# Zeroing the stacks of queries and keys on ScalarE instead of GpSimd in a two-layer attention kernel

## The chip, the cores and the metric

The kernel runs on one core of one Trainium2 chip, in one launch. The metric is device time in microseconds (us). The kernel before has a median of 918.5 us over 3 runs (918.21 to 922.14). The core's engines are named as in the profile: PE is TensorE's matmuls, PEld its weight loads, DVE is VectorE, ACT is ScalarE, POOL is GpSimd, SP is SyncE, whose queue issues the DMAs. Each engine works off its own instructions in the order in which they were written, and waits where an operand isn't there yet.

## The reference

Input `x` is 32 sequences of 256 tokens of 256 features, in float32. Two layers follow each other; each normalizes its input, attends, and modulates the outcome with a condition vector (512 features per sequence).

```python
# layer 0: linear attention, 8 heads of 32
xn = _ln(x, ln_w, ln_b)
q = softmax((xn @ Wq + bq).reshape(b, t, 8, 32), axis=-1)
k = softmax((xn @ Wk + bk + (1 - mask) * -1e6).reshape(b, t, 8, 32), axis=1)
v = ((xn @ Wv + bv) * mask).reshape(b, t, 8, 32)
att = einsum('bnhd,bnhl->bhdl', k, v)
y = einsum('bnhd,bhdl->bnhl', q, att)
# layer 1: softmax attention, 16 heads of 16
att = softmax(einsum('bnhl,bmhl->bnmh', q, k) + (1 - mask) * -1e6, axis=2)
y = einsum('bnmh,bmhl->bnhl', att, v)
# both, with their own weights
scale, shift = split(silu(emb) @ W_emb + b_emb)
x = x + silu(_ln(y, ln2_w, ln2_b) * (1 + scale) + shift) @ W_out + b_out
```

## The kernel before, in words

One function, `tile_two_layers`, first collects operations and then writes them out. `prepared()` lists the set-up: loading weights, folding the first normalization's weights into the projections, splitting float32 weights into a high and a low part (`w_high` on ACT, L305; `w_low` on DVE, L308), the modulation vectors, constants, and buffers that are filled once. `sequence(b)` lists the work of one of the 32 sequences (called batches here), in parts a (layer 0's attention), b (layer 0's output), c (layer 1's attention) and d (layer 1's output).

The order is written out by hand as numbers: `SET_UP` gives each set-up operation a place, `STARTS` each operation of a batch, to which `PERIOD` (26.2851) times the batch's number is added. `in_order` sorts all operations by place and runs them one after the other; an operation whose inputs or buffers aren't there yet is put off until they are. The places set the order of the instructions on every engine's queue. They are not clock times of a run.

Operations that stand near the change:

- `identity` (L264, POOL, place -708.56) makes the identity matrix `ident` and two small constants; `warmed` runs 16 transposes on PE with it; `identity_r` (L270 to L272, DVE) casts `ident` to `ident_r`, reduces it to `fold` and spreads that to `fold4`.
- `qk_zeros` (L507) fills one pair of stacks, `qs` and `ks`, with zeros; each is 128 partitions x 2048 float32 values. There are three pairs (`ROOM["qk"]`). The list in `SET_UP` goes by the order in which the operations are listed, but each `qk_zeros` takes the next pair when it runs, so the pair with the earliest place is the first to be used.
- `qk_made` (L512, places -52.44, 60.07, 77.11) then issues two DMAs from SP that write the constant rows into the pair's stacks (L515), and sets the pair free for use. In part c, the heads' queries and keys are copied by DMA into the other rows of a free pair (L991); rows that are not written stay zero, and the score matmuls (L1033, L1100) run over all of them.
- ACT's queue in the set-up: `w_high` of layer 0's output weights (`wout_hi`, place -439.51), `cond_tanh` (L425, place -332.9), `w_high` of layer 1's output weights (-231.47), and then the other `w_high` among the work of the first batches. DVE's queue there: `identity_r`, `token_terms` (L435, L436), one `w_rep` (L322, L323), `w_low` of layer 0's output weights (`wout_lo`, L308, reads `wout_hi`), the other `w_rep`, `bias_scaled` (L332). PE's `w_sums` (L345, L349) read the scaled bias and the spread rows of `w_rep`.
- The place 5.55 in ACT's queue lies between `split_high` of batch 0 (L752, place 4.18) and `k_kept` of batch 1 (L818, place 6.37). `k_kept` copies the turned keys of layer 0 into `kk`, which `attention` (L888, PE) reads; `k_sums` (L896) and `blocks` (L901) on DVE read its result, and `y_product` (L916, PE) reads theirs. After `k_kept` ACT has `high` and `whole` (L699, L703) of batch 3, and two `w_high`.

Of the kernel before, what the change touches and what calls it, by code (L numbers as in the profile page):

```python
# [10 lines left out]
F32 = mybir.dt.float32  # L11
# [5 lines left out]
P = 128  # L17
# [50 lines left out]
    identity_r=(-702.04,), load_bias=(-276.37,), load_bout=(-13.79, 53.66), load_cols=(-670.58,),  # L68
    load_cond=(-544.29,), load_emb=(-258.80, -217.52, -180.67, -207.44, -42.77, -14.95, -48.76, -2.89),
    load_masks=(-359.47,), load_w=(-291.77, -528.39, -390.22, -548.16, -39.72, -33.64, -88.51, -232.84),  # L70
    mask_terms=(-103.15,), p_made=(91.90, 5.63), qk_made=(-52.44, 60.07, 77.11), qk_zeros=(-61.21, -379.66,
    -674.55), qkp_made=(30.64,), terms0_store=(-141.84,), terms_rows=(-172.06,), terms_store=(-42.73,),
    terms_turn=(-333.70,), token_terms=(-574.41,), v0_made=(-369.51, -279.71), va_made=(-36.90, 52.97),
    w_high=(-50.10, -64.76, -198.98, -439.51, 25.73, 18.32, 14.13, -231.47), w_low=(-39.74, -58.97, -95.39,
    -307.80, 29.41, 24.14, 30.22, 4.56), w_rep=(-292.96, -366.10), w_scaled=(-76.66, -94.61, -210.46, 20.45,
# [89 lines left out]
def tile_two_layers(ctx: ExitStack, tc: tile.TileContext, a: dict, out: bass.AP):  # L165
# [11 lines left out]
    nc = tc.nc  # L177
    x = a["x"]
    B, S, D = x.shape
# [7 lines left out]
    NSLOT = NU * NC  # L187
# [4 lines left out]
    const = ctx.enter_context(tc.tile_pool(name="const", bufs=1))  # L192
# [8 lines left out]
    def f(ap):  # L201
        return ap.bitcast(F32)
# [6 lines left out]
    ident_r = const.tile([P, P], F32R, name="ident_r")  # L209
    fold = const.tile([P, B], F32, name="fold")  # L210
    one = const.tile([P, 1], F32, name="one")
    minus_half = const.tile([P, NBLOCK], F32, name="minus_half")
    fold4 = const.tile([P, P], F32, name="fold4")
    cols = const.tile([P, NCOL + 2 * NTOK], F32, name="cols")
# [26 lines left out]
    done = {}  # L241
# [11 lines left out]
    def prepared():  # L253
# [3 lines left out]
        def op(engine, time, run, *after, take=(), give=(), **more):  # L257
            ops.append(Op(engine, time, run, after, take, give, **(LATE.get(engine, {}) | more)))
            return ops[-1]
# [4 lines left out]
        def identity():  # L264
            make_identity(nc, ident)
            nc.gpsimd.memset(one, 1.0)
            nc.gpsimd.memset(minus_half, -0.5)

        def identity_r():
# [11 lines left out]

        o_cols = op("D", 0.3, load_cols)
        o = op("G", 0.9, identity)
        op("P", 0.11 * NWARM, warmed, o, take=("bank",), give=("bank",))
        done["ident"] = op("V", 0.13, identity_r, o)

# [153 lines left out]
        o = op("D", 0.3, load_bias)  # L440
# [17 lines left out]
        o = op("V", 0.2, token_terms, o_cols)  # L458
        o = op("P", 0.5, terms_turn, o, done["ident"], take=("bank",))
        o = op("V", 0.35, terms_rows, o, give=("bank",))  # L460
# [15 lines left out]
        o = op("D", 0.3, load_cond)  # L476
        o = op("A", 0.2, cond_tanh, o)
# [20 lines left out]
        o = op("D", 0.3, load_masks)  # L498
        o = op("V", 0.6, mask_terms, o)
# [7 lines left out]
        def qk_zeros():  # L507
            s.qk.append(qk_all.pop(0))
            for buf in s.qk[-1]:
                nc.gpsimd.memset(f(buf), 0.0)  # L510

        def qk_made():  # L512
            qk_bufs.append(s.qk.pop(0))
# [14 lines left out]
        o = op("G", 0.6, zero_one)  # L528
        o_stored = op("D", 0.3, zero_one_store, o)
        o_z = o_stored  # L530
        for n in range(ROOM["qk"]):
            o = op("G", 4.0, qk_zeros)
            o_z = op("D", 0.8, qk_made, o, o_z, give=("qk",))

        o_rep = norm_rows(1, o_cols)
# [630 lines left out]

    ctx.enter_context(tc.manual_schedule(engines=None))
    return in_order(prepared, [lambda b=b: sequence(b) for b in range(B)], ROOM)


# [67 lines left out]
```

## Time and profile before

| | |
|---|---|
| median of 3 runs | 918.5 us (918.21 to 922.14) |
| the profiled execution | 914.85 us, span 912.7 us |
| mean granted TensorE clock | 0.97 |
| PE busy | 864.9 us (95% of the span) |
| DVE busy | 813.5 us (89%) |
| ACT busy | 700.2 us (77%) |
| POOL busy | 692.4 us (76%) |
| the six zeroings on POOL, L510 | 1.80 to 1.82 us each; four from 1.80 to 8.84 us, two from 18.53 to 22.07 us |

The profile is that of one execution. The span is the time from its first to its last recorded instruction; the execution's own time is a little longer. A line of a timeline gives start and length in us, engine, source line, operation, the tile written and those read, the shape (partitions x elements) and how many were merged (x4); in brackets stands how long the engine was idle before and what ended it. The chain of waits is the work that ended last, followed backwards from the last instruction, at each step to what released it or to the instruction before it on its engine. In a table of stretches, each row gives the stretch, its length, the busy time of PE, PEld, DVE, ACT and POOL with their instructions, the granted TensorE clock (1.00 is full speed), the DMA engines' busy share and GB/s.

The page's slices (40 equal parts of the span, busy tenths) show where the time is filled and where it isn't:

```profile
PE   6878899999999999999999999999999999999973
DVE  6797989999999999999999999999999999999843
ACT  1365588788888898888888888888888888877762
POOL 5254567888888888988888888988888877775441
PEclk6799999999999999999999999999999999999985
```

The first four slices (about 91 us) and the last two are the start-up and the end; in between PE is busy nearly all the time.

### The profile page before, as it was taken

Reading aid. Unit: us, or ns where it says so; the run is one execution under the profiler, and the core shown is the slowest. Engines: PE = TensorE matmul, PEld = TensorE weight load, DVE = VectorE, ACT = ScalarE, POOL = GpSimd, SP = SyncE. Lnnn points to the kernel's source line nnn. Section 1 sums busy time; section 2 is a strip of 40 time slices with the busy share of each in tenths; the row PEclk is TensorE's granted clock in tenths of the full one; section 3 lists DMA queues with packets and bytes.
Section 4 is the critical chain, followed back from the end, with each engine's and each line's share of the span. In section 5 each row is a group of like instructions: output and inputs, shape, how many; then the busy total and the mean of one; then the engine's idle time right before and its main releaser. Section 6 shows DMA issues by size and latency. Waiting matters only on the chain.

```text
span 912.7 us, 25210 instructions
## 1 busy us (share of the span) xinstructions
PE 864.9 (95%) x9494; PEld 705.0 (77%) x9494; DVE 813.5 (89%) x2235; ACT 700.2 (77%) x1420; POOL 692.4 (76%) x893
## 2 busy tenths in 40 slices
PE   6878899999999999999999999999999999999973
PEld 3667787888888888888888888888888888877642
DVE  6797989999999999999999999999999999999843
ACT  1365588788888898888888888888888888877762
POOL 5254567888888888988888888988888877775441
PEclk6799999999999999999999999999999999999985
DMA  6302222322232222223222212332233221222200
GB/s 215 108 16 88 84 81 81 102 104 97 103 103 74 89 71 90 102 104 103 96 104 86 86 60 92 104 102 104 96 104 103 71 82 57 87 86 86 95 14 24
DMA packets 56767, 81.09 MB, mean 89 GB/s; under 512 B 5407, under 2 KB 30021, under 8 KB 56646
## 3 DMA queue, kind: packets, MB, share of 16 engines
q1 hardware_dynamic: 56646, 79.47, 25.4%
q8 instruction: 76, 1.25, 0.6%
q14 instruction: 45, 0.37, 0.1%
HBM read 19.52 MB, written 8.55 MB: 31 GB/s over the span
## 4 chain that ended last, share of the span: by engine, by line
PE 79%; DVE 15%; POOL 2%; issue 1%; ACT 1%; DMA 0%; POOLq 0%; DVEq 0%; ACTq 0%
PE bank L558 37%; PE bank L1122 12%; PE bank L1100 9%; PE bank L1033 8%; PE bank L565 5%; DVE mx L1044 5%; PE bank L916 3%; PE bank L814 1%; PE bank L888 1%; DVE st L591 1%; PE bank L650 1%; PE bank L349 1%; DVE th L746 1%; DVE ident_r L270 1%; DVE yb L1138 1%
## 5 line engine op out<-in xcount | busy, mean ns | idle before, releaser
L1044 DVE TENSOR_REDUCE mx<-bank 128x2 f32<-128x512 f32 x512 | 324.9, 673 | 15.0 <-PE bank L1033 14.7
L1113 ACT ACTIVATE p<-bank 128x512 f32<-128x512 f32 x512 | 270.2, 600 | 84.1 <-PE bank L1100 78.5
L558 PE MATMUL bank<-xh,w_hi 128*128 128x256 f32 x512 | 153.1, 299 | 0.1
L558 PE MATMUL bank<-xl,w_hi 128*128 128x256 f32 x512 | 144.3, 282 | 1.2 <-DVE xl L707 1.2
L558 PE MATMUL bank<-xh,w_lo 128*128 128x256 f32 x512 | 143.9, 281 | 0.0
L1122 PE MATMUL bank<-p,va 128*32 128x256 f32 x2048 | 140.0, 386 | 0.1
L558 PE MATMUL bank<-wout_hi,hp 128*128 128x256 f32 x512 | 112.9, 302 | 10.0 <-ACT hp L752 9.5
L982 POOL TENSOR_TENSOR qk_lo<-nrm,qk_hi 128x512 fp32r<-128x512 f32 x58 | 74.7, 1287 | 56.5 <-ACT nrm L978 56.5
L1100 PE MATMUL bank<-qs,ks 64*128 64x256 f32 x1024 | 109.0, 311 | 4.3 <-DMA qs<-m_row 3.1
L1033 PE MATMUL bank<-ks,qs 64*128 64x256 f32 x1024 | 105.4, 307 | 1.0 <-DVE mx L1044 0.3
L1100 PEld LDWEIGHTS bank<-qs,ks 64*128 64x128 f32 x1024 | 73.8, 187 | 37.0 <-ACT p L1113 22.6
L558 PEld LDWEIGHTS bank<-xh,w_hi 128*128 128x128 f32 x512 | 97.1, 190 | 5.1 <-DVE mx L1044 0.4
L558 PEld LDWEIGHTS bank<-xl,w_hi 128*128 128x128 f32 x512 | 97.3, 190 | 1.6 <-DVE xl L707 1.6
L558 PEld LDWEIGHTS bank<-wout_hi,hp 128*128 128x128 f32 x512 | 86.3, 196 | 15.6 <-ACT hp L752 10.1
L1033 PEld LDWEIGHTS bank<-ks,qs 64*128 64x128 f32 x1024 | 73.6, 185 | 31.3 <-issue 13.4
L558 PEld LDWEIGHTS bank<-xh,w_lo 128*128 128x128 f32 x512 | 96.9, 189 | 0.0
L613 POOL TENSOR_SCALAR nrm<-xt,mv,off 128x256 f32<-128x256 f32 x116 | 65.0, 571 | 29.0 <-DVE off L608 26.1
L1122 PEld LDWEIGHTS bank<-p,va 128*32 128x32 f32 x2048 | 55.0, 109 | 41.1 <-ACT p L1113 1.8
L728 POOL TENSOR_TENSOR xt<-xt,bout 128x512 f32<-128x512 f32 x64 | 82.5, 1288 | 3.1 <-DMA bout<-in_bout_dram 3.1
L756 POOL TENSOR_TENSOR hp<-th,hp 128x512 fp32r<-128x512 f32 x58 | 74.9, 1292 | 9.1 <-ACT hp L752 9.1
L558 PE MATMUL bank<-w_hi,xh 128*128 128x256 f32 x256 | 78.2, 305 | 0.0
L707 POOL TENSOR_TENSOR xl<-nrm,xh 128x512 fp32r<-128x512 f32 x58 | 73.6, 1288 | 4.3 <-ACT nrm L703 4.3
(138 smaller groups left out, 2153.9 us busy)
## 6 DMA issues: line engine op xcount, KB each, us to landing
ks<-qk_hi SPq DMA_DIRECT2D x64, 256.0 KB
qs<-qk_hi SPq DMA_DIRECT2D x64, 256.0 KB
xt<-in_x_dram SPq DMA_DIRECT2D x32, 256.0 KB
ks<-qk_lo SPq DMA_DIRECT2D x32, 256.0 KB
qs<-qk_lo SPq DMA_DIRECT2D x32, 256.0 KB
out_dram<-xt SPq DMA_DIRECT2D x32, 256.0 KB
mk<-t_dram SPq DMA_DIRECT2D x32, 128.0 KB
raw<-in_w_dram SPq DMA_DIRECT2D x8, 256.0 KB
```

The costliest lines, as they stand in the source:

```text
L558: nc.tensor.matmul(o, left, right, start=(n == 0), stop=(n == len(pairs) - 1))
L565: nc.tensor.transpose(ps[:, ds(c * S + t * P, P)], src[:, t, ts(c, P)], ident)
L613: (nc.vector if s.quick else nc.gpsimd).tensor_scalar(s.nrm[:, t, :], get()[:, t, :], s.mv[:, t, 1:2], s.off[:, t : t + 1], ALU.mult, ALU.add)
L707: engine.tensor_tensor(s.xp[1], s.whole, f(s.xp[0]), ALU.subtract)
L728: nc.gpsimd.tensor_tensor(s.x, s.x, bout[:, i : i + 1, :].to_broadcast([P, NT, D]), ALU.add)
L756: engine.tensor_tensor(s.hp[1], s.th, f(s.hp[0]), ALU.subtract)
L982: engine.tensor_tensor(s.qkp[1][:, :, c], s.qk_ps[c], f(s.qkp[0][:, :, c]), ALU.subtract)
L1033: nc.tensor.matmul(ps[w][:, ts(m, S)], s.qs[half(w), u, c, ts(m, P)], s.ks[half(w), u, c, :], start=True, stop=True,)
L1044: nc.vector.tensor_reduce(s.mx[:, :, w, u, c], halves(s.s_ps[0, c, u][w]), AX.X, ALU.max, negate=True)
L1100: nc.tensor.matmul(ps[w][:, ts(m, S)], s.ks[half(w), u, c, ts(m, P)], s.qs[half(w), u, c, :], start=True, stop=True,)
L1113: nc.scalar.activation(s.pt[c, u][:, w], s.s_ps[1, c, u][w], AF.Exp)
L1122: nc.tensor.matmul(s.yT_ps[c][32 * j : 32 * j + 32, ts(v, S)], s.va[:, m, 8 * c + 4 * v + j, :], s.pt[c, 2 * v + j // 2][:, j % 2, ts(m, S ...
```

## The change

The stacks are zeroed by ACT: `nc.scalar.copy` writes all 2048 columns of a stack from a new constant tile of one column, `nothing`, which POOL fills with zeros inside `identity`. `qk_zeros` becomes an operation of ACT's queue that needs `identity`; it has three new places in `SET_UP`, two of them near the set-up's start and one at 5.55. The operations around it, their places and the DMAs of `qk_made` stay.

```diff
@@ SET_UP
-    qk_zeros=(-61.21, -379.66, -674.55),
+    qk_zeros=(-650.21, -640.66, 5.55),
@@ tile_two_layers
     one = const.tile([P, 1], F32, name="one")
+    nothing = const.tile([P, 1], F32, name="nothing")
@@ identity
             nc.gpsimd.memset(one, 1.0)
+            nc.gpsimd.memset(nothing, 0.0)
             nc.gpsimd.memset(minus_half, -0.5)
@@ prepared
         o = op("G", 0.9, identity)
+        done["zero"] = o
@@ qk_zeros
             for buf in s.qk[-1]:
-                nc.gpsimd.memset(f(buf), 0.0)
+                nc.scalar.copy(buf.rearrange("p u c n -> p (u c n)"), nothing.to_broadcast([P, NSLOT * S]))
@@ prepared
         for n in range(ROOM["qk"]):
-            o = op("G", 4.0, qk_zeros)
+            o = op("A", 4.0, qk_zeros, done["zero"])
             o_z = op("D", 0.8, qk_made, o, o_z, give=("qk",))
```

More of the change, by code (lines that the diff above doesn't have):

```diff
@@ L70 @@
     load_masks=(-359.47,), load_w=(-291.77, -528.39, -390.22, -548.16, -39.72, -33.64, -88.51, -232.84),
-    mask_terms=(-103.15,), p_made=(91.90, 5.63), qk_made=(-52.44, 60.07, 77.11), qk_zeros=(-61.21, -379.66,
-    -674.55), qkp_made=(30.64,), terms0_store=(-141.84,), terms_rows=(-172.06,), terms_store=(-42.73,),
+    mask_terms=(-103.15,), p_made=(91.90, 5.63), qk_made=(-52.44, 60.07, 77.11), qk_zeros=(-650.21, -640.66,
+    5.55), qkp_made=(30.64,), terms0_store=(-141.84,), terms_rows=(-172.06,), terms_store=(-42.73,),
     terms_turn=(-333.70,), token_terms=(-574.41,), v0_made=(-369.51, -279.71), va_made=(-36.90, 52.97),
```

## The prediction

> **What bounds the kernel now.** I read the page first. The chain that ended last is PE for most of the span:
>
> ```profile
> PE 79%; DVE 15%; POOL 2%; issue 1%; ACT 1%; DMA 0%; POOLq 0%; DVEq 0%; ACTq 0%
> ```
>
> By the busy times of stretches, PE is busy 599.74 of the 600 us from 200 to 800. Nothing of the change runs there. What it can move is the start-up, where PE waits; a shift there reaches the end one for one if it lies on the chain. So I read the chain in order of time over the first 130 us, then the engines' timelines around each piece that the diff touches.
>
> ```profile
> 1.81 7.11 DVE ident_r L270
> 10.10 0.68 DVE wout_lo L308
> 11.70 1.21 PE bank L345 x2
> ```
>
> The columns are start and length in us. A cast of 128x128 takes 7.11 us and is on the chain. The timelines of POOL, DVE and ACT say why, and what stands beside it:
>
> ```profile
> 1.76 0.11 POOL L267 MEMSET minus_half<- 128x8 f32 x1
> 1.80 1.82 POOL L510 MEMSET qs<- 128x2048 f32 x1
> 7.02 1.82 POOL L510 MEMSET ks<- 128x2048 f32 x1
> 1.81 7.11 DVE L270 CAST ident_r<-ident 128x128 fp32r<-128x128 f32 x1 [0.29 <-POOL ident masks.py:199]
> 0.71 1.28 ACT L305 ACT_TABLE_LOAD   x1 [0.71 <-PEq L1225]
> 3.90 0.63 ACT L305 ACTIVATE wout_hi<-raw 128x512 fp32r<-128x512 f32 x1 [1.91 <-DMA raw<-in_w_dram]
> 4.44 0.29 ACT L425 ACTIVATE silu<-cond 128x128 f32<-128x128 f32 x1
> ```
>
> The cast starts with the four memsets of POOL and ends (8.92) just after the fourth (8.84): it is held by them, and with it all that DVE has queued. ACT meanwhile has done wout_hi by 4.53, so wout_lo (L308, reads wout_hi) at 10.10 waits for DVE alone.
>
> **The change at the start: a stall goes, another takes its place.** Four of the six zeroings go from POOL to the head of ACT's queue: their places, -650.21 and -640.66, come before the first w_high (-439.51) and cond_tanh (-332.9). DVE is free at about 2.1: the cast without the hold is some 0.2, as the 128x128 fill at L272 (0.23). That alone would be worth 6.8 us. But DVE works in order: it does L435, L436 and one w_rep (0.7 us in all), and then stands at wout_lo, which now waits for wout_hi, behind four zeroings on ACT. Behind wout_lo on DVE stand the second w_rep and bias_scaled, for which PE's w_sums (L345, 11.70) wait; on SP the loads from 10.81 on wait for wout_lo too, and shift with it.
>
> Price of one zeroing: no row has 128x2048 on ACT. The nearest are 128x512 SBUF to SBUF by the same call, the CAST of L752, 0.614 mean, and the 128x128 at L425, 0.293. From 128 to 512 elements (0.630 at L305) this is 0.88 ns an element: 0.614 + 1536 x 0.88 = 1.96 us. Two in a row of L305 take 1.15, so neighbours overlap by 0.11, and a zeroing displaces the next by 1.85. Low bound: the slope from 128x256 with a scale column (L840, 0.479) to L305, 0.59 ns, gives 1.52 and 1.41. High bound: the slope from 128x16 (L644, 0.188) to L425, 0.94 ns, gives 2.06 and 1.95. I take 1.96/1.85, whose rows have no pointer operands, like the new call.
>
> The table load: its row has line 305, that of the first ACTIVATE. Calls of scalar.copy show as CAST or COPY, not ACTIVATE (L752, L818), so I take it that the load stays in front of L305, now behind the four zeroings and no longer in the idle start. If it goes ahead of them it is covered as before; both ends are kept.
>
> Sum: the new memset of one column follows `one` on POOL and ends about 1.87 (row L267); zeroings from 1.89, end 1.89 + 3 x 1.85 + 1.96 = 9.40; table load to 10.68; wout_hi 0.63 to 11.31; wout_lo at 11.33 instead of 10.10: **+1.23**. With the load ahead: zeroings from 2.00 (1.99 ends the load), the last displaces wout_hi to 9.40, wout_lo at 10.05: -0.05. The 6.8 us won on DVE are thus given back to ACT's queue.
>
> The Trainium skill, ScalarE: Activation LUTs, section What ACT_TABLE_LOAD costs, speaks against the change harder than the rows: it gives 186 ns + 0.833 ns an element with immediates, an overlap of about 93 ns, and a drain of some 1380 ns on top of the load's 1283 ns. This trace shows 1283 ns, but before it nothing ran that could be drained. By the page, as an estimate, zeroings end at 9.18, load and drain at 11.84, wout_lo starts at 12.49, and the whole sum below would be +4.2 instead of +3.2.
>
> **The change at 51 us: two zeroings into a full stretch of ACT.** The third pair stood on POOL at 18.53 to 22.07, where POOL then idled 1.88 us and nothing waited: its removal gains nothing. Its new place, 5.55, lies between split_high of batch 0 (4.18) and k_kept of batch 1 (6.37). ACT and its followers there:
>
> ```profile
> 51.20 0.62 ACT L752 CAST hp<-th 128x512 fp32r<-128x512 f32 x1
> 51.72 0.58 ACT L818 COPY kk<-bank 128x512 f32<-128x512 f32 x1
> 53.57 0.46 PE L888 MATMUL bank<-v,kk 128*32 128x33 f32 x32
> 54.58 0.12 DVE L896 RECIPROCAL rk<-bank 128x2 f32<-128x2 f32 x1
> 55.15 1.15 PE L916 MATMUL bank<-att,eqT 64*128 64x66 f32 x16 [1.11 <-DVE att L901]
> ```
>
> kk moves by 2 x 1.85 = 3.70. Cover: kk ended at 52.30 and PE used it at 53.57, so 1.25 are hidden by the product before it (0.02 for the signal); the attention product then ended at 54.03 but DVE came to it at 54.58, another 0.53. Left: 3.70 - 1.25 - 0.53 = **+1.92** on rk, blocks (L901) and y_product (L916). The chain runs through exactly these:
>
> ```profile
> 54.74 0.36 DVE att L901
> 55.15 1.15 PE bank L916 x16
> 56.30 1.63 PE bank L558 x12
> ```
>
> and both PE and DVE carry on without a pause long enough to win it back (DVE next idles 0.23 at 59.65). The others behind the pair on ACT lose less: xh and whole of batch 3 (52.20, 52.78) are needed first by POOL's low part at 64.86; the two w_high (53.35) by DVE at 62.70; q_exp (57.92) follows DVE anyway. The qk_made DMAs keep their places on SP: the first (21.02) finds its pair zeroed at about 5.7, the second (81.88) at 9.4, the third (98.35) at about 57. The memset of `nothing` costs POOL 0.03 before PE's warm-up, which the long wait after 5.29 hides.
>
> **Sum.** +1.23 + 1.92 = +3.15 us, on the profiled 914.85 us (span 912.7): 918.0. That execution lies 3.65 below the median of the runs, 918.5; carried over, 921.65. By the bounds of a zeroing: 1.52/1.41 gives -0.53 + 1.04 = +0.5; 2.06/1.95 gives +1.63 + 2.12 = +3.75. So 919.0 to 922.3, and the runs before alone spread from 918.21 to 922.14.
>
> **Rivals.**
> *The table load goes ahead (20%).* -0.05 + 1.92 = +1.9: 920.4. For it: it ran at 0.71, as early as it could. Against: its line.
>
> *The shift is absorbed (10%).* 918.5, if what follows 55 us has slack that the chain doesn't show. Against it: the chain in order.
>
> *The stall's removal pays (5%).* If the zeroings ran after wout_hi, or were so short (under 0.5 us) that four fit before its data at 3.90, wout_lo would start at 4.55 and w_sums 1.60 later, at 6.2 (at the latest at 8.3, if the bias lands last: DMA share is 0.92 from 4 to 8, 0.07 after). Gain 3.4 to 5.5, less the 1.92: 914.9 to 917.0, and several us more if PE's clock then holds. Against it: the places in the queue and the low bound of 1.52.
>
> *The TensorE clock falls at 54 to 57 (15%), the slower side.* The clock of the stretches:
>
> ```profile
> 4.00:8.00 4.00, 1.30 (x8) 1.06 (x6) 4.00 (x2) 0.73 (x2) 4.00 (x3) 1.00 0.92 304
> 8.00:12.00 4.00, 0.91 (x3) 0.43 (x4) 3.43 (x17) 0.00 (x0) 0.84 (x1) 0.55 0.07 17
> 12.00:16.00 4.00, 4.00 (x9) 1.87 (x8) 1.04 (x3) 0.77 (x2) 0.00 (x0) 0.50 0.88 290
> 80.84 0.33 PE L565 MATMUL bank<-ident,nrm 128*128 128x128 f32 x1 [2.65 <-POOL nrm L613]
> ```
>
> The last number but two is the granted clock. An idle stretch of 4.28 us (5.29 to 9.57) cost it, one of 2.65 at 80.84 did not. The new gap for kk, from 53.65 to 56.02, is 2.4, but only 0.46 of small matmuls part it from 0.6 more: 3.4 in all. It decides from somewhere between 2.65 and 4.28 of idle. Price: y_product, the product, w_sums and k (1.15 + 1.63 + 0.62 + 1.07 + 1.6 = 6.1 us) at half clock, +6.1; the clock came back at 32.2, 2.6 after the dense products began at 29.54, so at least +2.6: 924.2 to 927.7.
>
> **How the numbers follow.** The forecast (load behind, clock kept) has 50%: 921.6. What this kernel's measurement can tell from no change is about 0.5%, 4.6 us. The forecast and the first two rivals lie inside it, but some of the forecast's share passes it by the spread of the runs: same 0.70. Slower 0.24: the clock, and that tail. Faster 0.06. The range, 916.5 to 926, takes in the gain's upper end and half of the clock's.
>
> **What would show it.** Right: six CASTs of 128x2048 at L513, near 1.9 us; L270 down to 0.2; wout_lo near 11.3 with the table load at 9.4; kk near 56.6 and y_product near 58.3; the clock 1.00 from 54 to 64; PE's time from 200 to 800 as it was. Wrong: w_sums before 9, a clock of 0.5 after 55, or a y_product that is not late.

## The result and the profile after

The changed kernel has a median of 922.52 us over 12 runs (920.81 to 924.74), the kernel before, run beside it, 918.98 us (915.78 to 924.63). The ratio is 1.0041, 95% interval [1.0025, 1.0057]: slower by 0.41%, some 3.8 us, inside what was called no change. The forecast was 921.6 with a range of 916.5 to 926. The profiled execution took 921.61 us (span 919.5). It lies 6.8 us above the profiled execution of the kernel before (914.85), which was quicker than all twelve timed beside the change; a length read between these two profiles can thus be off by some 3 us.

The chain that ended last, by engine, from the page of the changed kernel:

```profile
PE 81%; DVE 12%; ACT 3%; POOL 1%; issue 1%; DMA 1%; POOLq 0%; SPq 0%; ACTq 0%
```

ACT had 1% before and has 3% now, DVE went from 15% to 12%: a stretch of the chain moved from one engine to the other. The timelines of ACT, DVE and PE at the start of the changed kernel show which (start and length in us, engine, line, operation; in brackets the idle time before and what ended it):

```profile
0.71 1.28 ACT L513 ACT_TABLE_LOAD   x1 [0.71 <-PEq L1228]
2.01 1.90 ACT L513 CAST qs<-nothing 128x2048 fp32r<-128x2048 f32 x1
...
7.41 1.89 ACT L513 CAST ks<-nothing 128x2048 fp32r<-128x2048 f32 x1
9.21 0.62 ACT L308 ACTIVATE wout_hi<-raw 128x512 fp32r<-128x512 f32 x1
...
1.81 0.23 DVE L272 CAST ident_r<-ident 128x128 fp32r<-128x128 f32 x1 [0.29 <-POOL ident masks.py:199]
9.86 0.69 DVE L311 SCALAR_TENSOR_TENSOR wout_lo<-raw,wout_hi 128x512 fp32r<-128x512 f32 x1 [6.14 <-ACT wout_hi L308]
...
11.47 1.22 PE L348 MATMUL bank<-bias,ident 6*128 6x256 f32 x2 [5.80 <-DVE bias L335]
```

The cast of the identity takes 0.23 instead of 7.11 us. DVE then waits 6.14 us at wout_lo for wout_hi, which stands behind four zeroings. wout_lo starts at 9.86 (10.10 before), PE's first w_sums at 11.47 (11.70). The start is 0.2 us shorter, where the stall alone had cost 6.9. The table load stands ahead of the zeroings, not behind them.

The same engines at the third pair, 1.8 us later than the place was before, since hp itself came at 52.96 and not at 51.20:

```profile
52.96 0.62 ACT L755 CAST hp<-th 128x512 fp32r<-128x512 f32 x1 [1.82 <-DVE th L749]
53.49 1.89 ACT L513 CAST qs<-nothing 128x2048 fp32r<-128x2048 f32 x1
55.28 1.89 ACT L513 CAST ks<-nothing 128x2048 fp32r<-128x2048 f32 x1
57.08 0.57 ACT L821 COPY kk<-bank 128x512 f32<-128x512 f32 x1
57.71 0.67 PE L891 MATMUL bank<-v,kk 128*32 128x33 f32 x32 [3.99 <-ACT kk L821]
59.06 1.98 PE L919 MATMUL bank<-att,eqT 64*128 64x66 f32 x16 [0.69 <-DVE att L904]
64.24 1.13 PE L352 MATMUL bank<-raw,rep 128*128 128x256 f32 x4
```

The last group stood in the kernel before at

```profile
58.48 1.13 PE L349 MATMUL bank<-raw,rep 128*128 128x256 f32 x4
```

PE waits 3.99 us for kk, and then the attention product takes 0.67 where it took 0.46, and y_product 1.98 where it took 1.15. In this execution y_product starts 59.06 - 55.15 = 3.91 us later than in the profile before, of which about 1.8 come from the late hp (why it is late stands in the last section), and the last group 5.76 later. The stretches of the changed kernel show that the TensorE clock was at half (stretch, length, busy PE, PEld, DVE, ACT, POOL, then the granted TensorE clock, DMA share, GB/s):

```profile
52.00:56.00 4.00, 1.72 (x14) 1.50 (x12) 3.53 (x9) 3.04 (x3) 0.00 (x0) 1.00 0.00 0
56.00:60.00 4.00, 1.60 (x42) 1.47 (x42) 1.49 (x5) 3.86 (x6) 0.00 (x0) 0.56 0.00 0
60.00:64.00 4.00, 4.00 (x24) 3.65 (x22) 3.03 (x10) 0.63 (x1) 1.56 (x3) 0.59 0.01 2
```

The clock fell in the wait: 0.56 and 0.59 where the kernel before had 1.00. That was the rival with 15%, and a clock of 0.5 after 55 stood among the prediction's signs of being wrong. From 200 to 800 us PE is busy 599.76 of 600, as before (599.74).

### The profile page after: what moved, and what is told of

Same layout as the page of the kernel before. It is cut to its first block, busy times and chain, and to the rows that moved or that the text cites. A ratio compares the mean times of both kernels' runs of the same rounds, so it can differ in the third digit from the quotient of the medians.

```text
span 919.5 us, 25203 instructions
## 1 busy us (share of the span) xinstructions
PE 869.8 (95%) x9494; PEld 710.1 (77%) x9494; DVE 808.8 (88%) x2235; ACT 710.8 (77%) x1426; POOL 680.3 (74%) x888
## 3 DMA queue, kind: packets, MB, share of 16 engines
q8 instruction: 76, 1.25, 0.6%
## 4 chain that ended last, share of the span: by engine, by line
PE 81%; DVE 12%; ACT 3%; POOL 1%; issue 1%; DMA 1%; POOLq 0%; SPq 0%; ACTq 0%
PE bank L561 38%; PE bank L1125 12%; PE bank L1103 9%; PE bank L1036 8%; PE bank L568 5%; DVE mx L1047 4%; PE bank L919 3%; PE bank L817 1%; PE bank L891 1%; PE bank L653 1%; DVE st L594 1%; PE bank L352 1%; DVE th L749 1%; DVE yb L1141 1%; ACT qs L513 1%
```

## The experiments

Theory A: the place at 5.55 costs the time by the delay of kk. Theory B: beside the delay, the clock that falls in the wait. Theory C: the loss sits in the start. All kernels were timed in five rounds beside the kernel before; the ratios are against it, with 95% intervals. e1 to e4 ran on one chip, e5 to e8 on a second, e9 to e12 on a third.

| run | what | ratio | interval |
|---|---|---|---|
| the change | all three pairs on ACT, the third at 5.55 | 1.0041 | [1.0025, 1.0057] |
| e5 | the change again | 1.0029 | [1.0011, 1.0048] |
| e1 | third pair alone on ACT | 1.0034 | [1.0015, 1.0054] |
| e2 | first two pairs alone on ACT | 0.9992 | [0.9979, 1.0005] |
| e9 | the change, third pair at an idle place | 0.9975 | [0.9953, 0.9997] |
| e8 | the change, third pair zeroed twice | 1.0064 | [1.0042, 1.0087] |
| e4 | the change, 10 transposes in the wait for kk | 1.0010 | [0.9989, 1.0030] |
| e6 | the same, 24 transposes | 1.0014 | [0.9986, 1.0042] |
| e10 | the change, 48 transposes in the first wait | 0.9980 | [0.9955, 1.0005] |
| e3 | all pairs on ACT at idle places | 0.9941 | [0.9917, 0.9966] |
| e11 | e3 again | 0.9960 | [0.9936, 0.9984] |
| e7 | e3 with 24 transposes in the first wait | 0.9910 | [0.9883, 0.9938] |
| e12 | e7 again | 0.9911 | [0.9883, 0.9938] |

### One half of the change at a time: e1 and e2

In e1 the pairs that run first and second are zeroed by POOL at their old places; in e2 the last one is.

```diff
-    qk_zeros=(-650.21, -640.66, 5.55),
+    qk_zeros=(-674.55, -379.66, 5.55),      # e1; e2: (-650.21, -640.66, -61.21)
             for buf in s.qk[-1]:
-                nc.scalar.copy(buf..., nothing...)
+                if qk_all:                  # e2: if not qk_all
+                    nc.gpsimd.memset(f(buf), 0.0)
+                else:
+                    nc.scalar.copy(buf..., nothing...)
```

> Only the third pair is zeroed by ACT, at 5.55; the first two stay on POOL as before. Theory A (the place at 5.55 costs the time by delaying kk): slower than before by 1.8 us from the delay alone (2 x 1.80 less the 1.25 and 0.53 that were hidden), 1.0020. Theory B (the delay lets the TensorE clock fall at about 56): some 3.8 us or more, 1.004, with a granted clock of 0.5 to 0.6 from 56 to 62 in its profile. Theory C (the loss sits in the start): 1.000. The DVE cast of ident_r takes 7.1 us again.

> Only the first two pairs are zeroed by ACT, at the head of its queue; the third stays on POOL at its old place. Theories A and B: wout_lo at 9.9 as in the changed kernel against 10.1, so the time is that of before within 0.3 us, 0.9995. Theory C (the loss sits in the start, through the clock that is at half there): the whole loss, 1.004.

e1 has the loss, 1.0034; e2 has none, 0.9992. Theory C falls. The interval of e1 takes in both the 1.0020 of Theory A and the 1.004 of Theory B, so e1's time doesn't part these two. e1 is also the cleanest look at the delay, as its start is that of before and hp is on time (51.24):

```profile
51.75 1.91 ACT L515 CAST qs<-nothing 128x2048 fp32r<-128x2048 f32 x1
53.55 1.91 ACT L515 CAST ks<-nothing 128x2048 fp32r<-128x2048 f32 x1
55.35 0.59 ACT L823 COPY kk<-bank 128x512 f32<-128x512 f32 x1
55.99 0.46 PE L893 MATMUL bank<-v,kk 128*32 128x33 f32 x32 [1.05 <-ACT kk L823]
57.14 1.15 PE L921 MATMUL bank<-att,eqT 64*128 64x66 f32 x16 [0.69 <-DVE att L906]
58.82 0.63 PE L563 MATMUL bank<-wout_hi,hp 128*128 128x256 f32 x2
```

kk moved by 55.35 - 51.72 = 3.63, y_product by 57.14 - 55.15 = 1.99. The difference is what the product before and DVE's queue hid: 1.64 to the 1.78 of the forecast. Part of Theory B's sign is there too. The attention product and y_product run at full speed, but the product behind them doesn't: two of its matmuls take 0.63, where the kernel before had

```profile
56.56 0.40 PE L558 MATMUL bank<-wout_hi,hp 128*128 128x256 f32 x2
```

and the granted clock of e1 is 0.77 from 56 to 60 and 0.80 from 60 to 64. The clock fell here behind waits of only 1.05 and 0.69 us.

### The place, not the engine: e9

```diff
-    qk_zeros=(-650.21, -640.66, 5.55),
+    qk_zeros=(-650.21, -640.66, -15.0),
```

> The changed kernel with the third pair's place alone moved, from 5.55 to -15, where ACT idles before q_exp of batch 1. Theory A and B (the place, not the engine, is what costs): the time of the run in which POOL kept the third pair, 0.999. A theory by which ACT is too full for six zeroings wherever they stand: 1.003 to 1.004 as with the change.

0.9975, an interval that doesn't touch that of the change. The pair now runs from 39.34 to 43.03, and ACT still idles 3.10 us behind it before q_exp. ACT can carry all six without a loss; at 5.55 it can't carry two.

### The delay doubled: e8

```diff
             for buf in s.qk[-1]:
-                nc.scalar.copy(buf..., nothing...)
+                for again in range(2 if not qk_all else 1):
+                    nc.scalar.copy(buf..., nothing...)
```

> The changed kernel with the third pair zeroed twice over at 5.55. Nothing hides the second pair, so Theory A gives another 3.6 us: 1.008. Theory B the same, and up to 3 us more where the clock falls in a longer wait, 1.008 to 1.011. If the place isn't on the path, 1.004 as before.

1.0064, 0.0035 above the change beside it (e5): 3.2 us by the ratios (2.7 by the medians) for the 3.6 of two more zeroings. It is less than the 1.008 or more that the theories gave, though the interval reaches 1.008, and it overlaps that of e5 a little (1.0042 to 1.0048). A holds for the direction and about the size. The waiting of PE is longer, and the clock is down again behind it:

```profile
48.92 3.83 ACT L514 CAST qs<-nothing 128x2048 fp32r<-128x2048 f32 x2
52.65 3.82 ACT L514 CAST ks<-nothing 128x2048 fp32r<-128x2048 f32 x2
57.01 0.67 PE L892 MATMUL bank<-v,kk 128*32 128x33 f32 x32 [6.17 <-ACT kk L822]
58.36 1.98 PE L920 MATMUL bank<-att,eqT 64*128 64x66 f32 x16 [0.68 <-DVE att L905]
```

### The clock in the wait for kk: e4, e6, with e5 beside e6

Transposes of the identity that nothing reads, on PE between the product of batch 2 and the attention product of batch 1; ten in e4, 24 in e6. e5 is the changed kernel as it is.

```diff
+        def filled():
+            ps = bank()
+            for n in range(10):             # e6: 24
+                nc.tensor.transpose(ps[:, ts(n % 4, P)], ident, ident)
+        op("P", 2.1, filled, o, take=("bank",), give=("bank",))   # place 12.6
```

> The changed kernel with ten transposes of ident (nothing reads them) on PE between the product of batch 2 and the attention product of batch 1, where PE waits for kk: 2.1 us of work in a gap of 2.3. Theory B (clock): the clock stays 1.00 from 56 to 64 and about half of the loss goes, 1.002. Theory A (delay alone): the loss stays what it is with the change, 1.004, or grows by a few tenths.

> The changed kernel as it is, as the measure for the others beside it on one chip: 1.004 against before by all theories.

> The changed kernel with 24 transposes (about 3 us at the 0.12 that one took) in PE's wait for kk, where ten took 1.25. Theory B (part of the loss is the clock that falls in the wait): attention and the products behind it run at full speed in more of the executions, 1.001 or less, at least 0.002 under the changed kernel beside it. Theory A (delay alone): the changed kernel's 1.004 or more.

In e4 the ten took 1.25 us and left a wait of 1.96, and what follows ran at full speed:

```profile
54.38 1.25 PE L292 MATMUL bank<-ident 128*128 128x128 f32 x10
57.59 0.46 PE L898 MATMUL bank<-v,kk 128*32 128x33 f32 x32 [1.96 <-ACT kk L828]
58.83 1.11 PE L926 MATMUL bank<-att,eqT 64*128 64x66 f32 x16 [0.79 <-DVE att L911]
62.12 1.13 PE L359 MATMUL bank<-raw,rep 128*128 128x256 f32 x4
```

From the attention product to this last group is 62.12 - 57.59 = 4.53 us; in the changed kernel's profile it is 64.24 - 57.71 = 6.53, in e5's 6.82, in e6's 4.54, before 4.91. The half clock costs 1.6 to 2.3 us in this stage of a profiled execution. In the whole time the fillings point the same way, 1.0010 and 1.0014 against 1.0041 and 1.0029, but the intervals overlap, and e6 missed both the 1.001 and the 0.002 that were asked of it: in its profile the 24 transposes end 1.0 us after kk is ready (56.07), and so hold the attention product up themselves. How often the clock falls there, and so its share in the median, stays open.

### The zeroings at idle places: e3 and e11

```diff
-    qk_zeros=(-650.21, -640.66, 5.55),
+    qk_zeros=(-320.0, -150.0, -15.0),
```

> All six zeroings on ACT, but at places where ACT idled before: -320 (behind cond_tanh), -150 (behind the w_high of -198.98) and -15 (behind whole of batch 2). If ACT's queue is what gives the 6.8 us of DVE back, wout_lo starts near 4.6 and w_sums between 6.2 and 8.3 instead of 11.7, and kk isn't delayed: faster by 3.4 to 5.5 us, 0.994 to 0.996. If the clock then doesn't fall before w_sums either, up to 10 us more. If the start has other limits (loads, clock), 1.000.

> The zeroings at idle places once more, beside the next kernel on one chip: 0.994.

0.9941 and 0.9960: 5.4 and 3.7 us faster than before, near what the 6.8 us of the stall, less what waits anyway, let expect. From e3's timelines:

```profile
4.08 0.63 ACT L307 ACTIVATE wout_hi<-raw 128x512 fp32r<-128x512 f32 x1 [2.09 <-DMA raw<-in_w_dram]
4.75 0.69 DVE L310 SCALAR_TENSOR_TENSOR wout_lo<-raw,wout_hi 128x512 fp32r<-128x512 f32 x1 [0.95 <-ACT wout_hi L307]
7.66 0.28 DVE L334 TENSOR_SCALAR bias<-bias 6x256 f32<-6x256 f32 x1 [1.53 <-DMA bias<-in_bias_dram]
8.00 1.22 PE L347 MATMUL bank<-bias,ident 6*128 6x256 f32 x2 [2.07 <-DVE bias L334]
9.14 2.08 PE L351 MATMUL bank<-raw,rep 128*128 128x256 f32 x4
```

wout_lo starts at 4.75; the bias is late next, its load lands at 7.66; w_sums begins at 8.00 instead of 11.70. It still runs at half speed: four matmuls of L351 take 2.08, later in the kernel 1.13.

It is not shown that the 3.7 us won at the start are the gain of the whole. e9, whose zeroings at the head still hold wout_hi, is itself at 0.9975, and beside it on one chip e11 is lower by only 0.0015, with overlapping intervals. The profiles can't tell: the profiled executions (917.48 and 917.25) were the longest of e3 and e11, and in them y_product of batch 1 starts at 55.07 and 54.99, against 55.15 before, after a clock of 0.50 from about 35 to 45 us.

### The clock in the first wait: e7, e12 and e10

The same transposes, between those of the token terms and the first w_sums: 24 in the kernel with the idle places (e7, e12), 48 in the changed kernel (e10, whose wait is longer).

```diff
+        op("P", 3.0, filled, o, take=("bank",), give=("bank",))   # place -300; e10: 5.6
```

> The zeroings at idle places (0.994) and 24 transposes on PE between the transposes of the token terms and the first w_sums, where PE waits from 5.9 to 8.0. If the idle wait there is what sets the first w_sums to half speed (2.08 for four matmuls at L351 against 1.13 later), they run at full speed and the start shrinks by 3 to 8 us: 0.986 to 0.991. If the speed is set by something else, 0.994 or a little above, as w_sums starts up to 1 us later.

> The zeroings at idle places with the 24 transposes ahead of the first w_sums once more: 0.991. If the transposes are worth what full speed from 8 to 20 us lets expect, at least 2 us under the kernel without them; if the two can't be told apart, the idle places alone did it.

> The changed kernel with 48 transposes on PE (5.6 us at 0.117) in its wait for the first w_sums, 5.7 to 11.5. If the idle wait sets the stage from 11.5 to 23 to half speed, that stage takes 5 to 6 us less and L352 shows 1.13 instead of 2.08; what follows waits for DVE and loads for part of it: 0.997 to 1.000 (1.0035 of the change less 3 to 6 us). If not, 1.004.

e7's PE:

```profile
5.23 2.78 PE L291 MATMUL bank<-ident 128*128 128x128 f32 x24
8.04 0.69 PE L354 MATMUL bank<-bias,ident 6*128 6x256 f32 x2
8.67 1.13 PE L358 MATMUL bank<-raw,rep 128*128 128x256 f32 x4
...
13.10 1.05 PE L397 MATMUL bank<-raw,silu 128*32 128x512 f32 x4
```

w_sums runs at full speed: the first three of them take 13.10 - 8.04 = 5.06 us, where the kernel before took 21.15 - 11.70 = 9.45. e7 and e12 are at 0.9910 and 0.9911, medians of 909.72 and 911.21 us. Beside e11 on one chip, e12 is lower by 0.0049, some 4.5 us (2.7 by the medians); the intervals just overlap, and e7 and e3, which ran on two chips, lie the same way apart (0.9910 and 0.9941). e10 says it once more without the idle places: 0.9980 against the change's 1.0029 and 1.0041. It wasn't the wait of 2.07 us in e3 that took a full clock away: there the sixteen warm-up transposes took 3.67 us, 0.23 each, and ran at half speed to their end, where e7's 24 took 2.78, 0.12 each. The further transposes bring the array to full speed (in e12 the clock's first record, of 1.00, is at 6.62 us, in the midst of them) or keep it there (in e7 it is at 4.70, just ahead of them). The transposes alone in the kernel before were not tried.

## Why the prediction held, step by step

The time lay near the forecast partly by luck: two of its steps were wrong, with opposite signs.

- **The stall moves to ACT's queue: right.** Four zeroings at the head hold wout_hi, DVE stands at wout_lo, and SP's loads shift with it (10.58 against 10.81).
- **A zeroing at 1.96, neighbours at 1.85: a little high.** Measured 1.89 and 1.80. The Trainium skill, ScalarE: Activation LUTs, section What ACT_TABLE_LOAD costs, gives 186 ns + 0.833 ns an element, with 93 ns of overlap between neighbours; worked out for 2048 elements this is an estimate of 1.89 and 1.80. Here the page was nearer than the rows.
- **The table load behind the zeroings, +1.23: wrong.** It stands ahead of them, with line 513, that of the first zeroing, though those are CASTs and not ACTIVATEs. The start is -0.24 instead. The reading that a CAST wouldn't draw the load to itself was the step that failed; the rival with 20% had it right. wout_lo started at 9.86 instead of 11.33. The drain of some 1380 ns that the page gives with a switch of tables doesn't show: the first zeroing starts at 2.01, 0.02 after the load's end, and nothing ran before the load that could be drained.
- **The wait for kk, +1.92: right.** e1 has 1.99 on y_product. In the profile of the change itself it is 3.91, with the late hp in it, which the forecast didn't have.
- **The clock kept at 54 to 57: wrong in the executions that were profiled.** Its price there was 1.6 to 2.3, under the 2.6 to 6.1 of the rival. The wait was put at 2.4, and was 3.99 in the change and 3.04 in e5, where hp too came late, and 6.17 in e8 with the pair zeroed twice. The forecast decided by the length of the wait, between 2.65 and 4.28; e1, where 1.05 and 0.69 were enough, shows that the length alone doesn't decide it.
- **The sum:** -0.24 + 1.99 + 1.6 to 2.3 is 3.4 to 4.1, for a measured 3.8 (e5: 2.7). The clock's part in it is that of profiled executions; what it is in the median isn't shown. As far as it goes, the forecast's 3.15 was near since the table load, 1.5 too much, made up for the clock, which was left out. The place and the delay of kk were right, the size by luck.
- **The rival that the stall's removal pays:** its condition was that the zeroings run after wout_hi. e3 sets it, and gives 5.4 and, again in e11, 3.7 us where 3.4 to 5.5 less 1.92 had been worked out for the change; without the third pair's delay the 1.92 falls away. How much of this is the start isn't settled, as e9 shows.

## What to carry to other kernels

An operation that holds another engine up is only worth moving if the new queue has room at that place: read what stands behind it there, and choose an idle stretch of that engine, since engine and place are two changes and here the place decided the sign. A wait of PE can cost more than its length, because the work behind it may run at half speed, and its length alone doesn't tell whether it will; a few idle matmuls in a wait can be worth more than the wait itself, as in e12, or run past its end and hold the next product up, as in e6. Where two terms of a forecast are uncertain in opposite directions, a near total says little of either.

## What the runs showed of the hardware

Behind waits of PE of 3.04, 3.99 and 6.17 us (e5, the change, e8) the next matmuls ran at half speed, behind waits of 1.96 (e4) and 2.65 us (before, at 80.84) at full. But in e1 waits of 1.05 and 0.69 us were followed by half speed from 58.2 on. The recorded clock shows why a length doesn't settle it: it changes only at certain moments. In the first 75 us of the changed kernel these are 5.27, 8.68, 22.34, 35.99, 46.23, 56.47, 63.30, 70.12 and 73.53 us, all whole multiples of 3.41 apart; every run here has the same step, from another first moment (4.95 before, 6.12 in e4, 4.70 in e7). In the 3.41 us ahead of a fall PE was busy for 0.66 us in the change (fall at 56.47), 0.87 in e5 (57.13), 0.58 in e8 (53.67) and 1.67 in e1 (58.17); in e4 it was busy for 1.72 up to 57.33, and the clock held. So the same wait may or may not cost the clock, by how it lies to these moments. There is no sharp limit in these figures: before, 1.56 us up to 80.04 were enough. That this makes the spread of one kernel's times is likely, but not shown.

Once down, the array stayed at half speed through more than 9 us in which PE was busy without a pause: L352 took 2.08 us three times from 12.62 to 21.01 in the changed kernel. The clock came back at 22.34.

The granted clock of a stretch isn't always what the matmuls ran at. In e3 the stretch from 12 to 16 us is recorded at 1.00, and its matmuls took the 2.08 us of half speed. The trace has no record of the clock there before 28.32, and a stretch ahead of the first record reads 1.00 here:

```profile
12.00:16.00 4.00, 4.00 (x8) 2.17 (x8) 3.21 (x13) 3.84 (x3) 0.91 (x2) 1.00 0.91 310
12.29 2.08 PE L351 MATMUL bank<-raw,rep 128*128 128x256 f32 x4
```

The length of a known matmul is the better witness.

POOL holds DVE up in small places too. In e5, DVE's operations on 32 and 64 columns take 1.3 us instead of 0.24 and 0.18 beside POOL's operations of 128x512, and end with them, which makes th and so hp late:

```profile
48.70 1.35 DVE L412 SCALAR_TENSOR_TENSOR add<-scale,cols,shift 128x32 f32<-128x32 f32 x1
49.97 1.31 DVE L413 TENSOR_SCALAR mul_h<-mul 128x64 f32<-128x64 f32 x1
48.72 1.28 POOL L710 TENSOR_TENSOR xl<-nrm,xh 128x512 fp32r<-128x512 f32 x1
49.96 1.27 POOL L731 TENSOR_TENSOR xt<-xt,bout 128x512 f32<-128x512 f32 x1
```

The same is seen in e2, whose time is not longer than before, so it isn't the loss by itself.
